# A two-layer network in fp32 on one core: Lora's products beside the convolutions, other accumulators for the outer products, and rows ordered by batch

## The chip, the cores and the metric

The kernel runs on one core of one Trainium2 chip. The metric is device time in microseconds of one execution, the median of several. Engines are named as the profile does: PE is TensorE (matmuls; PEld are its weight loads), DVE VectorE, ACT ScalarE, POOL GpSimd, SP SyncE, which here only starts DMAs.

## What is computed

x has 128 images of 64 channels with 1024 positions, in fp32. Two residual layers follow each other:

```
# layer 0: a 1x1 convolution whose weight is mixed for each image, then a low-rank product along the positions
att  = softmax(mlp(cond));  agg_w = einsum('bk,koi->boi', att, W);  agg_b = att @ bias_k
x = x + (einsum('boi,bih->boh', agg_w, x) + agg_b) @ (A @ B.T).T + bias
# layer 1: a grouped convolution (9 taps, 4 groups of 16 channels) plus a context of the image ...
y = conv1d(x, w9, groups=4, padding=4) + ctx[:, :, None] + s[None, :, None]
# ... then W_up (1024 x 1024) and the Lora product of the expert with the largest logit
base  = y @ W_up.T
delta = lora_B[e] @ (lora_A[e] @ y),   e = argmax(y @ gate_w.T + expert_bias)
x = x + base + delta
```

## The kernel before, in words

Two images (2 x 64 channels = 128 rows) are a pair `pr`, two pairs are a tile of rows `r`, and two tiles are a group `d`: 64 pairs, 32 tiles, 16 groups. All engines' orders are written out by hand (`manual_schedule`), so the order of statements is the order on each engine's queue. Within a group the loop over d (from L1005 on) weaves three things.

**W_up in seven products.** The product with W_up is done in the Strassen way: a group's y is a 2 x 2 of blocks, and seven outer products (`Outer`, i = 0 to 6), each again a Winograd scheme of seven inner products, replace eight and eight. POOL forms the sums of y: `gather` (S, L634) and `inner` (s0 to s3, L649). An inner product (`product`, L653) is two matmuls of 128 rows by 256 columns, which fp32 turns into four in the profile; in outer products 0 to 3 some are 292 wide, since 36 columns of the gate and of lora_A ride along. The accumulators are four PSUM banks: `pa` in a pool with one buffer, and `t0` to `t2`, of which an outer product takes two in turn (`product_bank`, L124). ACT copies one accumulator onto another (L686, L697, L706) and the fifth product aside (v, L694), DVE adds v and adds the accumulators to the rows of x (`evict`, L666; the helper `combine`, L211, records all these). `rest` (L689) calls the next outer product's `first` before its own last product, and `hooks` at the points a to d, where other work is put in. `spread` (L684) copies `first`'s product into `pa`, so it waits until DVE has emptied the one `pa`.

**Layer 0 and the convolution of the next group.** `in_rows` (L804: 8 accumulating products per pair, L480), `mix_rows` (L795, L490), `out_rows` (L799: two 512-wide products per pair, L511, added to x by DVE, L512). x then goes to DRAM (L513) and comes back (L520, L521) with 8 phases and 16 channels on the partitions, into one of three tiles X. `conv_rows` (L780) then fills six PSUM banks: `shared_in` twice (pm, L556: 8 matmuls of 64 by 128 each, 16 in the profile), `conv_in` four times (pc, L594, fed by POOL's `differences`, L548 and L549), with `shared_out` (m, L571 on DVE, copied to the other half by ACT, L574) between them, and at the end four `conv_out` (yt, L606 on DVE). A convolution's matmul writes 128 neighbouring columns of its bank, one group after the other, and y's rows hold the two images as neighbours, so that `conv_out` writes every eighth element.

**Gate and Lora.** After the second outer product of a pair (0 and 1, 2 and 3) `gate` (L725) picks the expert on DVE, in the free columns of one of the t banks; `turn` (L754) transposes the chosen part on PE, and `lora` (L761) makes four products of 32 rows by 512 columns (L766) into four banks, which DVE adds to x (L768). Then the rows go out (`store`, L770).

Everything else in PSUM (pxb, pz, pd, pm, pc, pzt, pl) takes the banks of the pool `ps`, of which there are four. In the loop the order on PE was: outer 0, in_rows, outer 1, out_rows, outer 2, in_rows, Lora of the first tile, outer 3, out_rows, outer 4, conv_rows of the next group's first tile, outer 5, Lora of the second tile, outer 6, conv_rows of the next group's second tile.

Of the kernel before, what the change touches and what calls it, by code (L numbers as in the profile page):

```python
# [41 lines left out]
P = 128  # L42
# [54 lines left out]
def block(ctx: ExitStack, tc: tile.TileContext, a: dict, out: bass.AP):  # L97
# [5 lines left out]
    psa = ctx.enter_context(tc.tile_pool(name="psa", bufs=1, space=PSUM))  # L103
# [17 lines left out]
    T = [pst.tile([P, N], F32, tag=f"t{i}", name=f"t{i}") for i in range(3)]  # L121
    turns = [0]

    def product_bank():  # L124
        turns[0] += 1
        return T[(turns[0] - 1) % 3]

# [171 lines left out]
    nc.gpsimd.memset(att, 0.0)  # L299
    ones = const.tile([P, 8], F32, name="ones")  # L300
    nc.gpsimd.memset(ones, 1.0)
    rank = const.tile([P, E], F32, name="rank")
    for e in range(E):
        nc.gpsimd.memset(rank[:, e : e + 1], float(E - e))

    sel = const.tile([P, FIRST, CH, 2], F32, name="sel")
    nc.vector.tensor_copy(
        sel,
        ident[:, : 2 * FIRST].rearrange("p (t b) -> p t b", b=2).unsqueeze(2).to_broadcast([P, FIRST, CH, 2]),
# [6 lines left out]
    def load_cond(g):  # L316

        if g * GP >= FIRST:
            bds[g] = BD[g % NBD]
            for b in range(2):  # L320
                nc.sync.dma_start(
                    bds[g].rearrange("(r two) t b o -> two r t b o", two=2)[b, :, :, b, :],
                    aggd.rearrange("(t two) r o -> two r t o", two=2)[b, :, g * GP : (g + 1) * GP],
                )
            load_rows(g, aggbs, aggbd, "ab")
# [21 lines left out]
    def spare(j, name):  # L347

        if j == 0:
            return psa.tile([P, N], F32, tag="pa", name=name)  # L350
        return T[j - 1]

# [48 lines left out]
    def own_att(pr):  # L401

        p = bank(f"pattx{pr}")
        nc.tensor.matmul(p[:, :8], sel[:, pr].rearrange("p o b -> p (o b)"), att[:, 0, :8], start=True, stop=True)
        attx[pr] = const.tile([P, 8], F32, name=f"attx{pr}")
        nc.vector.tensor_copy(attx[pr], p[:, :8])
# [78 lines left out]
    def layer0_mix(pr):  # L485
# [6 lines left out]
        to = z0.rearrange("k (o b) -> k b o", b=2)  # L492
        pzv = pz[:, :P].rearrange("k (b o) -> k b o", b=2)
# [7 lines left out]
    def layer0_out(pr, then=None, later=False):  # L501
        x, z0 = xs[pr], z0s.pop(pr)
        xt = X[pr % NX]
        d = x1d.tile([Q, P, P], F32, tag="x1d", name=f"x1d{pr}")
        dv = d.rearrange("q (c g) m -> (q c) g m", g=BG)
        h = P // 2
        for hf in range(2):
            cols = slice(hf * 512, (hf + 1) * 512)
            qs = slice(hf * Q // 2, (hf + 1) * Q // 2)
            pd = bank(f"pd{pr}_{hf}")  # L510
            nc.tensor.matmul(pd, z0, at[:, cols], start=True, stop=True)  # L511
            nc.vector.tensor_tensor(x[:, cols], pd, x[:, cols], ALU.add)  # L512
            nc.sync.dma_start(  # L513
                d[qs].rearrange("q r m -> r q m"), x[:, cols].rearrange("r (q m) -> r q m", m=P)
            )
        if then:
            then()

        def back():
            nc.sync.dma_start(xt[h:, :, :P], dv[:h])  # L520
            nc.sync.dma_start(xt[:h, :, 1 : P + 1], dv[h:])  # L521

        if later:
            return back
        back()

    def blocks(pr, b, g, first):

        skip = first // 2
        run = X[pr % NX][:, 2 * g + b, skip : skip + P]  # L530
        return run.rearrange("p (m two) -> p two m", two=2)[:, first - skip]

    def by_group(v):
        return v.rearrange("m (g q o) -> m g q o", g=NGC, q=Q)

    def context(pr, b, rows=slice(0, P)):
        v = ctxs[pr // GP][rows, pr % GP, b].rearrange("m (g o) -> m g o", g=NGC)
        return v.unsqueeze(2).to_broadcast([v.shape[0], NGC, Q, GC])
# [12 lines left out]
    def shared_in(pr):  # L551

        pm = bank(f"pm{pr}")
        for g in range(NGC):
            for b in range(2):
                nc.tensor.matmul(  # L556
                    pm[b * H : (b + 1) * H, g * P : (g + 1) * P],
                    blocks(pr, b, g, 1),
                    wsum[:, g],
                    start=True,  # L560
                    stop=True,
                )
        pms[pr] = pm

    def shared_out(pr):
# [3 lines left out]
        for b in range(2):  # L569
            half = slice(b * H, (b + 1) * H)  # L570
            nc.vector.tensor_tensor(by_group(m2[half, b]), by_group(pm[half]), context(pr, b, half), ALU.add)  # L571
# [5 lines left out]
    def conv_in(pr, b):  # L577

        pc = pcs[pr, b] = bank(f"pc{pr}_{b}")
        for g in range(NGC):  # L580
            cols = slice(g * P, (g + 1) * P)
            if pr < PLAIN:
                for s in range(2):
                    for o in range(2):
                        nc.tensor.matmul(
                            pc[o * H : (o + 1) * H, cols],
# [5 lines left out]
            else:  # L592
                for o in range(2):
                    nc.tensor.matmul(  # L594
                        pc[o * H : (o + 1) * H, cols],
                        diffs[pr][:, 2 * g + b, o],
# [5 lines left out]
    def conv_out(pr, b):  # L602
        if pr % 2 == 0 and b == 0:
# [3 lines left out]
            yt.rearrange("m q (o g two) -> m two g q o", two=2, g=NGC)[:, b],  # L607
            by_group(pcs.pop((pr, b))),
            context(pr, b) if pr < PLAIN else by_group(m2s[pr][:, b]),
# [8 lines left out]
    class Outer:  # L618
        def __init__(self, d, i):
            self.d, self.i, self.n = d, i, NG if i < GATES else NQ  # L620
            self.name = f"{d}_{i}"
            self.last_of_gate = i < GATES and i % 2 == (1 if d else 0)

# [31 lines left out]
        def gated(self, k, p):  # L655
            if self.i < GATES:
                r = self.i // 2
                if self.last_of_gate:
                    to = gate_part(r, 0, 3 * GL)
                else:  # L660
                    if r not in zslots[self.d]:
                        zslots[self.d][r] = sp.tile([P, 3 * GL], F32, tag="zs", name=f"zs{self.d}_{r}")
                    to = zslots[self.d][r]
# [14 lines left out]
        def first(self):  # L678
            self.t1 = product_bank()
            if self.last_of_gate:  # L680
                gate_bank[self.i // 2] = T[turns[0] % 3]
            self.product(self.t1[:, : self.n], self.unit(0, 0), held(self.i, 0), True)

        def spread(self):  # L684
            self.pa = psa.tile([P, N], F32, tag="pa", name=f"pa{self.name}")
            nc.scalar.copy(self.pa[:, :NQ], self.t1[:, :NQ])  # L686
            self.gated(2, self.t1)

        def rest(self, then, hooks):  # L689
            self.t2 = product_bank()  # L690
            wt = WT[self.i]
            self.product(self.t2[:, :NQ], self.s[0], wt[:, 1], True)
            v = tmp.tile([P, NQ], F32, tag="v", name=f"v{self.name}")
            nc.scalar.copy(v, self.t2[:, :NQ])  # L694
            hooks("a")
            self.product(self.pa[:, :NQ], self.s[1], wt[:, 2])
            nc.scalar.copy(self.t2[:, :NQ], self.pa[:, :NQ])  # L697
            hooks("b")
            self.product(self.t1[:, : self.n], self.unit(0, 1), held(self.i, 1))
            self.gated(0, self.t1)  # L700
            self.evict(self.t1[:, :NQ], 1)
# [3 lines left out]
            self.product(self.t2[:, : self.n], self.s[2], held(self.i, 2))  # L705
            nc.scalar.copy(self.pa[:, NQ:], self.t2[:, :NQ])  # L706
            both = self.pa.rearrange("p (k n) -> p k n", k=2)
            combine(nc.vector, both, both, "+", v.unsqueeze(1).to_broadcast([P, 2, NQ]))
# [3 lines left out]
            self.product(self.t2[:, : self.n], self.unit(1, 1), held(self.i, 3))  # L712
            if then:
                then.spread()
            self.gated(1, self.t2)
            self.evict(self.t2[:, :NQ], 2)

    zslots = {}
    gate_bank = {}

    def gate_part(r, first, n):

        return gate_bank[r][:, NG + first : NG + first + n]

    def gate(d, r):  # L725

        zs = zslots[d].pop(r)
        z = gate_part(r, 0, 3 * GL)
        z2 = sp.tile([P, GL], F32, tag="z2", name=f"z2{d}_{r}")
        nc.vector.tensor_tensor(z2, z[:, 2 * GL :], zs[:, 2 * GL :], ALU.add)  # L730
        nc.vector.tensor_tensor(z[:, : 2 * GL], z[:, : 2 * GL], zs[:, : 2 * GL], ALU.add)
        nc.vector.tensor_tensor(z[:, GL : 2 * GL], z[:, GL : 2 * GL], z2, ALU.add)  # L732
        pv = z[:, : 2 * GL].rearrange("p (t n) -> p t n", t=2)
        lg, sc = (gate_part(r, 3 * GL + 2 * E * k, 2 * E).rearrange("p (t e) -> p t e", t=2) for k in range(2))
# [45 lines left out]
    def conv_rows(r):  # L780

        a, b = pairs(r)
        shared_in(a)
# [115 lines left out]
    zslots[0] = {}  # L899
# [6 lines left out]
    o[0, 1].spread()  # L906
    o[0, 1].rest(o[0, 0], steps(wb[0], {"a": 1, "b": 2, "c": 2, "d": 1}))
# [8 lines left out]
    conv_rows(1)  # L916
# [11 lines left out]
    o[0, 3].spread()  # L928
    wb[2] = w_block(2, (0, 1, 3))
# [65 lines left out]
    zslots[1] = {}  # L995
# [9 lines left out]
    for d in range(1, ND):  # L1005
        more = d + 1 < ND
        r0, r1 = 2 * d + 2, 2 * d + 3
        if more:
            for i in range(7):
                o[d + 1, i] = Outer(d + 1, i)  # L1010
            zslots[d + 1] = {}
# [22 lines left out]
        else:  # L1034
            conv_rows(2 * d + 1)
# [9 lines left out]
        zms[0] = gate(d, 0)  # L1045
        if more:
            out_rows(r0)

# [11 lines left out]
        q[2].rest(q[3], hook({"c": [turn0]} if more else {}))  # L1060
        if more:
            in_rows(r1)
            lora(d, 0, zts[0])
# [8 lines left out]
        zms[1] = gate(d, 1)  # L1072
        if not more:
            lora(d, 0, zts[0])
        if more:
            back = out_rows(r1, True)

# [10 lines left out]
        q[4].rest(q[5], hook({"c": [turn1]} if more else {}))  # L1088
        if more:
            conv_rows(r0)  # L1090
            back()

# [19 lines left out]
        q[5].rest(q[6], nothing)  # L1112
        if d + 2 < ND:
            lora(d, 1, zts[1])
# [8 lines left out]
        q[6].rest(o[d + 1, 0], nothing)  # L1123
        if d + 2 < ND:
            store(d, 1)
            conv_rows(r1)
        else:
            lora(d, 1, zts[1])
            store(d, 1)


def _by_rows(v):

    v = v.reshape(2, NGC, GC, *v.shape[2:])
    return np.moveaxis(v, (2, 1, 0), (0, 1, 2)).reshape(P, *v.shape[3:])
# [93 lines left out]
```

## Time and profile before

| what | value |
|---|---|
| median of 3 runs (lowest to highest) | 1224.99 us (1223.98 to 1226.67) |
| the profiled execution's own time | 1229.31 us |
| span in its profile | 1227.3 us |
| PE, DVE, POOL, ACT busy | 98%, 68%, 64%, 26% of the span |
| granted TensorE clock | 0.997 of full |
| DMA | 277.58 MB, mean 226 GB/s |

The profile comes from one execution, which took 1229.31 us; the span lies within it. A line of the time line gives start and duration in us, engine, line of the kernel, operation, written and read tiles, partitions x elements of the operands, and how many instructions are merged into it; in square brackets stands how long the engine was idle before it and what ended that. Ends of matmuls are modelled, so start to start tells more of PE than durations do.

### The profile page before, as it was taken

The page shows a single profiled execution, that of the slowest core. Times are in us where ns is not written, and L with a number is a line of the kernel's source. Part 1 is how long each engine was busy: PE and PEld are TensorE (multiplying, and loading weights), DVE is VectorE, ACT ScalarE, POOL GpSimd, SP SyncE. Part 2 cuts the span into 40 slices and gives each one's busy share as a digit, 9 for nine tenths or more (in the row PEclk, how much of TensorE's full clock was granted, in tenths as well). Part 3 has the DMA queues.
Part 4 walks back from the last instruction along what each step waited for, and adds up shares of the span by engine and source line. Part 5 has one row for each costly group of instructions (what it writes and reads, how often), then busy time and mean ns, then how long its engine had stood idle before and what let it go on. Part 6 is the DMA issues. An engine that isn't in the chain of part 4 may idle for free.

```text
span 1227.3 us, 22059 instructions
## 1 busy us (share of the span) xinstructions
PE 1204.6 (98%) x8007; PEld 967.5 (79%) x8007; DVE 833.4 (68%) x1699; ACT 314.7 (26%) x927; POOL 786.8 (64%) x749
## 2 busy tenths in 40 slices
PE   8889999999999999999999999999999999999998
PEld 6756878888787888878888787788878878788876
DVE  6768757676675767667676675767667576675765
ACT  3324322222132222213222232222213222132221
POOL 2478568756667676567756657766567756657753
PEclk9989999999999999999999999999999999999999
DMA  8976877677786677777677686767777676686633
GB/s 297 290 281 167 277 236 225 224 221 247 217 247 204 186 278 210 232 240 228 224 218 252 208 258 206 209 249 205 232 243 224 230 216 253 206 245 219 178 134 132
DMA packets 200939, 277.58 MB, mean 226 GB/s; under 512 B 18304, under 2 KB 159232, under 8 KB 200832
## 3 DMA queue, kind: packets, MB, share of 16 engines
q1 hardware_dynamic: 168304, 127.12, 36.9%
q10 hardware_dynamic: 32528, 149.06, 35.3%
q8 instruction: 64, 1.05, 0.4%
q14 instruction: 43, 0.35, 0.1%
HBM read 201.36 MB, written 74.78 MB: 225 GB/s over the span
## 4 chain that ended last, share of the span: by engine, by line
PE 90%; DMA 4%; issue 2%; DVE 2%; POOL 1%; ACT 1%; SPq 0%; ACTq 0%; DVEq 0%; POOLq 0%
PE t L653 40%; PE pa L653 15%; PE pxb L480 9%; PE pd L511 9%; PE pc L594 8%; PE pm L556 4%; PE pl L766 3%; DMA X<-x1d 1%; PE pz L490 1%; DMA wp<-in_wq 1%; POOL s L211 1%; DMA x1d<-xr 1%; DMA ctxd<-ctx 1%; POOL S L211 1%; DVE xr L211 0%
## 5 line engine op out<-in xcount | busy, mean ns | idle before, releaser
L211 DVE TENSOR_TENSOR xr<-xr,t 128x256 f32<-128x256 f32 x384 | 146.9, 417 | 148.3 <-ACT t L664 103.5
L653 PE MATMUL pa<-wt,s 128*128 128x256 f32 x896 | 230.4, 380 | 1.6 <-POOL S L211 1.3
L775 POOL TENSOR_TENSOR xr<-xr,ffn_bias 128x1024 f32<-128x1024 f32 x61 | 142.7, 2362 | 137.9 <-DVE xr L211 66.9
L211 POOL TENSOR_TENSOR S<-yt,yt 128x1024 f32<-128x1024 f32 x48 | 113.6, 2366 | 153.9 <-PE t L653 153.9
L653 PEld LDWEIGHTS pa<-wt,s 128*128 128x128 f32 x896 | 165.2, 190 | 32.3 <-issue 2.4
L211 DVE TENSOR_TENSOR pa<-pa,v 128x512 f32<-128x512 f32 x112 | 78.3, 699 | 139.6 <-ACT pa L706 139.6
L653 PE MATMUL t<-wp,S 128*128 128x256 f32 x576 | 142.7, 379 | 0.4 <-ACT pa L706 0.4
L480 PEld LDWEIGHTS pxb<-B,xt 128*128 128x128 f32 x1024 | 122.9, 196 | 12.4 <-DVE t L732 5.3
L480 PE MATMUL pxb<-B,xt 128*128 128x128 f32 x1024 | 124.0, 280 | 6.5 <-DVE t L732 4.9
L211 DVE TENSOR_TENSOR xr<-xr,pa 128x512 f32<-128x512 f32 x192 | 124.8, 684 | 3.9
L653 PEld LDWEIGHTS t<-wp,S 128*128 128x128 f32 x576 | 109.5, 190 | 17.4 <-ACT pa L706 0.8
L653 PE MATMUL t<-wt,s 128*128 128x256 f32 x448 | 121.8, 394 | 1.3 <-POOL s L211 1.2
L606 DVE TENSOR_TENSOR yt<-pc,m 128x512 f32<-128x512 f32 x124 | 121.3, 1100 | 1.0
L211 POOL TENSOR_TENSOR s<-S 128x256 f32<-128x256 f32 x160 | 116.6, 729 | 5.2
L653 PEld LDWEIGHTS t<-wt,s 128*128 128x128 f32 x448 | 78.8, 190 | 51.4 <-issue 38.6
L511 PE MATMUL pd<-AT,z 128*128 128x512 f32 x256 | 116.8, 596 | 1.5 <-ACT z L496 0.8
L548 POOL TENSOR_TENSOR df<-X 128x512 f32<-128x512 f32 x62 | 64.6, 1043 | 81.7 <-DMA X<-x1d 48.3
L594 PE MATMUL pc<-ws,df 128*64 128x128 f32 x1984 | 114.3, 273 | 1.5 <-DVE wg L211 1.1
L653 PE MATMUL t<-wg,S 128*128 128x292 f32 x384 | 111.2, 413 | 0.5 <-POOL S L211 0.5
L768 DVE TENSOR_TENSOR xr<-pl,xr 128x512 f32<-128x512 f32 x128 | 79.5, 683 | 46.8 <-PE pl L766 46.8
L594 PEld LDWEIGHTS pc<-ws,df 128*64 128x64 f32 x1984 | 109.4, 137 | 2.3 <-POOL df L549 1.3
L653 PE MATMUL t<-wg,yt 128*128 128x292 f32 x384 | 110.2, 410 | 0.5 <-ACT pa L706 0.5
(147 smaller groups left out, 1670.7 us busy)
## 6 DMA issues: line engine op xcount, KB each, us to landing
wt<-wd ACTq DMA_DIRECT2D x105, 768.0 KB, 4.7
x1d<-xr SPq DMA_DIRECT2D x128, 256.0 KB, 3.5
X<-x1d SPq DMA_DIRECT2D x128, 256.0 KB, 4.3
out<-xr SPq DMA_DIRECT2D x31, 1024.0 KB, 6.9
xr<-in_x ACTq DMA_DIRECT2D x28, 1024.0 KB, 7.8
xt<-in_xt ACTq DMA_DIRECT2D x55, 512.0 KB, 8.6
wd<-wt ACTq DMA_DIRECT2D x7, 768.0 KB, 4.7
xt<-in_xt SPq DMA_DIRECT2D x9, 512.0 KB, 7.0
```

Source lines behind the costliest of these rows:

```text
L211: eng.tensor_tensor(to, x, y, ALU.add if op == "+" else ALU.subtract)
L480: nc.tensor.matmul(pxb[:, :P], xt[:, c, :], bt[:, c, :], start=(c == 0), stop=(c == NC - 1))
L490: nc.tensor.matmul(pz[:, :P], xbs.pop(pr), bd.rearrange("p b o -> p (b o)"), start=True, stop=not first)
L511: nc.tensor.matmul(pd, z0, at[:, cols], start=True, stop=True)
L548: nc.gpsimd.tensor_tensor(diffs[pr][:, :, 0], at_even, at_odd, ALU.subtract)
L556: nc.tensor.matmul(pm[b * H : (b + 1) * H, g * P : (g + 1) * P], blocks(pr, b, g, 1), wsum[:, g], start=True, stop=True,)
L594: nc.tensor.matmul(pc[o * H : (o + 1) * H, cols], diffs[pr][:, 2 * g + b, o], ws[:, g, o], start=True, stop=True,)
L606: nc.vector.tensor_tensor(yt.rearrange("m q (o g two) -> m two g q o", two=2, g=NGC)[:, b], by_group(pcs.pop((pr, b))), context(pr, b) if ...
L653: nc.tensor.matmul(p, lhs[:, c], w[:, c], start=fresh and c == 0, stop=c == 1, skip_group_check=True)
L766: nc.tensor.matmul(p, zt[rows, :], lb[rows, :], start=True, stop=True)
L768: nc.vector.tensor_tensor(x, p, x, ALU.add)
L775: eng.tensor_tensor(xs[pr], xs[pr], fbias, ALU.add)
```

## The change

- **Accumulators.** `psa` is gone. The fourth bank is U, which all outer products share; an outer product's `t` turns through the three T, and its `pa` is the T that the one before used as `t`. The product that uses `pa` comes first in `rest`, the product for v (`fifth`) goes to a bank of `ps` and moves behind the second use of `t`. The gate's parts accumulate in U over two products (ACT zeroes them first in outer products of an even or odd number, by group), and the gate works in a bank of `ps`, with one DVE operation less and some small ACT copies more.
- **Order.** In the loop, conv_rows of the next group's first tile moves behind outer product 5, and both Loras move directly ahead of a conv_rows (their first `pm` then goes to U). Outer product 5 follows 4 directly. `gate` moves behind `out_rows`, its transpose from hook c to hook d. In the last group there is no such convolution, and Lora stays between outer products. The first group's order stays, but for the place of `fifth`.
- **Rows.** x's, y's and the context's rows are ordered image, channel in group, group. A convolution's matmul now writes every fourth column of its bank, the groups interleaved; `conv_out` writes runs of 64 elements. x goes to DRAM by image (two DMAs per pair, as before, but after both halves have been added), and comes back in four DMAs per pair in place of two.

The diff, cut to its core:

```diff
-    psa = ctx.enter_context(tc.tile_pool(name="psa", bufs=1, space=PSUM))
     T = [pst.tile([P, N], F32, tag=f"t{i}", name=f"t{i}") for i in range(3)]
+    U = pst.tile([P, N], F32, tag="u", name="u")
...
-            nc.sync.dma_start(
-                d[qs].rearrange("q r m -> r q m"), x[:, cols].rearrange("r (q m) -> r q m", m=P)
-            )
+        for b in range(2):
+            nc.sync.dma_start(
+                d[b].rearrange("q c g m -> (c g) q m"),
+                x[b * CH : (b + 1) * CH].rearrange("r (q m) -> r q m", m=P),
+            )
...
         def back():
-            nc.sync.dma_start(xt[h:, :, :P], dv[:h])
-            nc.sync.dma_start(xt[:h, :, 1 : P + 1], dv[h:])
+            for b in range(2):
+                dv = d[b].rearrange("q c g m -> (q c) g m")
+                own_ = slice(b * NGC, (b + 1) * NGC)
+                nc.sync.dma_start(xt[h:, own_, :P], dv[:h])
+                nc.sync.dma_start(xt[:h, own_, 1 : P + 1], dv[h:])
...
+    def by_phase(v):
+        return v.rearrange("m (q n) -> m q n", q=Q)
+
+    def of_group(v, g):
+        return v.rearrange("m (n g) -> m g n", g=NGC)[:, g]
...
-                    pm[b * H : (b + 1) * H, g * P : (g + 1) * P],
+                    of_group(pm[b * H : (b + 1) * H], g),
                     blocks(pr, b, g, 1),
                     wsum[:, g],
-                    start=True,
+                    start=g == 0,
...
-                        pc[o * H : (o + 1) * H, cols],
-                        diffs[pr][:, 2 * g + b, o],
+                        of_group(pc[o * H : (o + 1) * H], g),
+                        diffs[pr][:, NGC * b + g, o],
...
         nc.vector.tensor_tensor(
-            yt.rearrange("m q (o g two) -> m two g q o", two=2, g=NGC)[:, b],
-            by_group(pcs.pop((pr, b))),
-            context(pr, b) if pr < PLAIN else by_group(m2s[pr][:, b]),
+            yt[:, :, b * CH : (b + 1) * CH],
+            by_phase(pcs.pop((pr, b))),
+            context(pr, b) if pr < PLAIN else by_phase(m2s[pr][:, b]),
...
         def first(self):
-            self.t1 = product_bank()
+            k = turns[0]
+            turns[0] += 1
+            self.t, self.pa = T[k % 3], T[(k - 1) % 3]
...
+        def fifth(self):
+            m5 = bank(f"m5{self.name}")
+            self.product(m5[:, :NQ], self.s[0], WT[self.i][:, 1], True)
+            self.v = tmp.tile([P, NQ], F32, tag="v", name=f"v{self.name}")
+            nc.scalar.copy(self.v, m5[:, :NQ])
...
         def rest(self, then, hooks):
-            self.product(self.t2[:, :NQ], self.s[0], wt[:, 1], True)
-            nc.scalar.copy(v, self.t2[:, :NQ])
-            hooks("a")
             self.product(self.pa[:, :NQ], self.s[1], wt[:, 2])
-            nc.scalar.copy(self.t2[:, :NQ], self.pa[:, :NQ])
+            nc.scalar.copy(U[:, :NQ], self.pa[:, :NQ])
+            if self.first_of_gate:
+                nc.scalar.copy(U[:, NQ:NG], none)
+            hooks("a")
+            self.product(self.t[:, : self.n], self.unit(0, 1), held(self.i, 1))
+            self.gated(0, self.t)
+            self.evict(self.t[:, :NQ], 1)
             hooks("b")
-            self.product(self.t1[:, : self.n], self.unit(0, 1), held(self.i, 1))
-            self.gated(0, self.t1)
-            self.evict(self.t1[:, :NQ], 1)
+            if not self.v:
+                self.fifth()
             hooks("c")
...
-    def conv_rows(r):
+    def conv_rows(r, first=U):
         a, b = pairs(r)
-        shared_in(a)
+        shared_in(a, first)
...
-        zms[0] = gate(d, 0)
         if more:
             out_rows(r0)
+        zms[0] = gate(d, 0)
...
-        q[2].rest(q[3], hook({"c": [turn0]} if more else {}))
+        q[2].rest(q[3], hook({"d": [turn0]} if more else {}))
         if more:
             in_rows(r1)
-            lora(d, 0, zts[0])
...
-        q[4].rest(q[5], hook({"c": [turn1]} if more else {}))
-        if more:
-            conv_rows(r0)
-            back()
-
+        q[4].rest(q[5], hook({"d": [turn1]} if more else {}))
...
         q[5].rest(q[6], nothing)
+        lora(d, 0, zts[0])
+        conv_rows(r0)
+        back()
         if d + 2 < ND:
-            lora(d, 1, zts[1])
             load_cond(r0 + 2)
...
         q[6].rest(o[d + 1, 0], nothing)
+        lora(d, 1, zts[1])
+        store(d, 1)
         if d + 2 < ND:
-            store(d, 1)
             conv_rows(r1)
```

## Prediction, made before the changed kernel was run

> **What bounds the kernel now.** I read the page first (busy shares, slices, chain), then the busy time of each engine in three stretches, then TensorE's waits in the middle stretch, then the time line around the places that the change moves.
>
> ```profile
> PE 1204.6 (98%) x8007; PEld 967.5 (79%) x8007; DVE 833.4 (68%) x1699; ACT 314.7 (26%) x927; POOL 786.8 (64%) x749
> ...
> PE 90%; DMA 4%; issue 2%; DVE 2%; POOL 1%; ACT 1%; SPq 0%; ACTq 0%; DVEq 0%; POOLq 0%
> ```
>
> The first line is the engines' busy time, the second the chain of work that ended last, by engine. The next is the stretch from 174 to 1129 us: its length, then busy time (and instructions) of PE, PEld, DVE, ACT and POOL, granted clock, DMA share, GB/s.
>
> ```profile
> 174.00:1129.00 955.00, 955.00 (x6422) 773.29 (x6421) 644.88 (x1313) 235.20 (x702) 632.13 (x585) 1.00 0.74 228
> ```
>
> PE is busy for all of its 955 us, DVE for 645, POOL for 632; asked for PE's waits in that stretch, the trace lists none. So thirteen periods (one per group d; the same rows come back every 73.5 us) hold no gap on PE. Nothing is won there by making another engine faster; a change gains only if PE's own stream gets shorter, and any wait that it adds is paid in full. Since matmul ends are modelled, I go by starts.
>
> **What Lora costs today.** The rows: start, duration, engine, line.
>
> ```profile
> 642.85 1.89 PE L653 MATMUL t<-wp,S 128*128 128x256 f32 x8
> ...
> 644.67 1.14 PE L766 MATMUL pl<-lb,zt 32*128 32x512 f32 x8
> ...
> 645.74 1.13 PE L653 MATMUL t<-wt,s 128*128 128x256 f32 x4
> 645.83 2.49 DVE L768 TENSOR_TENSOR xr<-pl,xr 128x512 f32<-128x512 f32 x4 [0.63 <-PE pl L766]
> ...
> 646.71 1.03 PE L653 MATMUL pa<-wt,s 128*128 128x256 f32 x4
> ```
>
> An undisturbed product of four 256-column matmuls takes 0.86 to 0.87 us from start to start (617.37 to 618.23 in the next rows). Lora's matmuls use 32 of the 128 rows of the array, four at once. Entering costs 644.67-642.85-2x0.865 = 0.09 us, the products 1.07 (645.74-644.67), and the first full product after them takes 0.97, so leaving costs 0.11. That is 1.27 us for the second Lora of a group. The first one stands behind layer0_in and needs banks that ACT still empties; its rows are these:
>
> ```profile
> 614.93 1.55 PE L766 MATMUL pl<-lb,zt 32*128 32x512 f32 x8
> 616.40 1.13 PE L653 MATMUL t<-wt,s 128*128 128x256 f32 x4
> 617.37 1.03 PE L653 MATMUL pa<-wt,s 128*128 128x256 f32 x4
> 618.23 1.15 PE L653 MATMUL t<-wg,S 128*128 128x292 f32 x4
> ```
>
> It takes 1.47 plus 0.09 and 0.11, that is 1.67. In both, DVE starts adding the four results 1.16 us after the first matmul (645.83-644.67) and is at it for 2.49 us.
>
> **What a convolution costs today.**
>
> ```profile
> 633.04 1.97 PE L556 MATMUL pm<-wsum,X 128*64 128x128 f32 x32
> ...
> 633.74 0.74 DVE L211 TENSOR_TENSOR xr<-xr,t 128x256 f32<-128x256 f32 x2
> ...
> 634.41 2.84 DVE L571 TENSOR_TENSOR m<-pm,cx 64x512 f32<-64x512 f32 x4
> ...
> 634.84 3.66 PE L594 MATMUL pc<-ws,df 128*64 128x128 f32 x64
> ...
> 637.27 3.92 DVE L606 TENSOR_TENSOR yt<-pc,m 128x512 f32<-128x512 f32 x4
> ...
> 638.43 1.13 PE L653 MATMUL t<-wt,s 128*128 128x256 f32 x4
> ```
>
> Six banks are filled, 0.90 us each: two pm, then four pc. The sixth takes the bank of the second pm, so it waits until DVE's fourth m is done. It starts at 633.04+5x0.90 = 637.54, m ends at 634.41+2.84 = 637.25: hidden, with 0.29 us to spare. What happens without that cover is in the last group, where DVE began later:
>
> ```profile
> 1175.02 2.81 PE L594 MATMUL pc<-ws,df 128*64 128x128 f32 x48
> 1175.19 2.84 DVE L571 TENSOR_TENSOR m<-pm,cx 64x512 f32<-64x512 f32 x4
> ...
> 1178.18 1.10 PE L594 MATMUL pc<-ws,df 128*64 128x128 f32 x16 [0.34 <-DVE m L571]
> ```
>
> m ends at 1178.03, PE goes on at 1178.18: 0.15 us from DVE's end to PE. PE was due at 1175.02+3x0.90 = 1177.72, so it lost 0.46.
>
> **Part 1, Lora directly ahead of conv_rows** (14 first Loras, d = 1 to 14; 13 second ones, d = 1 to 13). One change of array shape goes away on each side, and the first Lora no longer waits for ACT: without a new wait the pair would take 1.07 + s + 5.40 us, s being the direct change from row tiles to column tiles, in place of 1.67 or 1.27 plus 5.40. The trace has no such change; the nearest rows give 0.09 to 0.11, nothing is the other end. But DVE's four additions now stand in its queue ahead of the four m. With Lora's first matmul at 0: additions 1.16 to 3.65; m from 3.57 (DVE overlaps such operations by 0.07, as 633.74+0.74 against 634.41) to 6.41; the sixth bank from 6.56. In the changed program the sixth bank is still that of the second pm; the first pm goes to U, which DVE has emptied by then (the like operation before a convolution ends at 634.48 above, and with one destination in place of two still 0.3 earlier, against 1.07 us of Lora on PE). PE alone would be there at 1.07+s+4.50 = 5.57+s, so s is hidden up to 0.99, and PE waits. From Lora's start to the sixth bank: 6.56, against 4.50 plus the old Lora: 6.56-4.50-1.67 = +0.39, and 6.56-4.50-1.27 = +0.79. Sum: 14x0.39 + 13x0.79 = **+15.7 us**. The other banks come free in time (the last addition ends at 3.65, the fifth bank is due at 4.67).
>
> **Part 2, the accumulators.** Matmul counts stay. Outer products 4 and 5 now follow each other directly, so the cover of a convolution is gone there. By the rows: pa's copy (ACT, 0.36) starts 0.25 after its product, ends at 0.61 and reaches PE 0.15 later, inside the 0.86 of the product between. DVE's chain for one outer product (v added 0.70, two 512-wide and two 256-wide additions) ends 3.3 us after the product that starts it; the copy into U waits for it and is done at 3.9, and the first product that needs it is due at 4.3. So no new stall: 0, but at slacks of 0.1 to 0.4. In the last group, which has no filler, the old rotation stalls:
>
> ```profile
> 1187.14 1.10 PE L653 MATMUL pa<-wt,s 128*128 128x256 f32 x4 [0.28 <-ACT zs L664]
> ...
> 1194.23 1.10 PE L653 MATMUL t<-wt,s 128*128 128x256 f32 x4 [1.19 <-POOL s L211]
> ...
> 1210.81 1.10 PE L653 MATMUL pa<-wt,s 128*128 128x256 f32 x4 [1.34 <-POOL S L211]
> ```
>
> By starts these are 0.45, 1.36 and 1.50 us late. The first and third wait for the copy into pa behind DVE's additions, and go; of the second about 0.9 goes, since it hangs on POOL, whose input the shorter conv_out gives 1.4 us earlier. **-2.9 us.** The gate loses one DVE operation (0.19) and moves behind layer0_out: DVE ends it at about 6.4 us after pd's first matmul, its transpose is due at 6.9, hidden. ACT gains small copies; it is at 26%.
>
> **Part 3, batch outermost.** conv_out writes runs of 64 in place of every eighth element: four take 3.92 us now, four contiguous ones of that size 2.49 (the additions above). That spares DVE 1.4 us per convolution, 45 in all, after the wait of part 1, so it is worth 0. POOL's differences keep their size. The way back from DRAM takes 4 DMAs per pair of images in place of 2: 128 more issues on SP at 0.52 us each, which delay store and load_cond behind them by 1 us; the store is still issued over 10 us before the load into its rows. X of the fourth pair lands some 5 us after the first pm, 8 us before its use. 0; in the first 100 us, where DMA is 88% busy, up to 1 us either way.
>
> The price that no row shows is pm and pc written to PSUM at every fourth element. Lower end: no change, 0.90 us a bank (below nothing is excluded: as many columns pass). Upper end: as DVE fares in SBUF, 3.92/2.49 = 1.57 times, 1.41 us a bank. Lora's start to the sixth bank is then 1.07+5x1.41 = 8.12, and that bank 0.51 longer: +2.46 and +2.86 a pair, 14 and 13 times, and 6x0.51 for each of the 4 convolutions without Lora, +84 in all. I take the lower end: the nearest row is that of the same matmuls into the same memory, DVE's has another engine and another memory, and up to 1.2 times is hidden behind the DVE wait anyway (5x1.08+1.07 = 6.5).
>
> Against it stands a rule of the Trainium skill, "PSUM — Partial Sum Buffer", Specifications: PSUM's lines are 8 bytes, and any non-contiguous pattern slows matmuls significantly. No run here shows it; if it doubles a bank's time (an estimate from two fp32 values to a line), the sum is +156 in place of +13.
>
> **Sum.** The profiled execution took 1229.31 us (span 1227.3), 4.3 above the median of the three runs, 1224.99. +15.7-2.9 = +12.8: 1242.1 for such an execution, **1238** for the median.
>
> **Rivals.**
> *No wait at the sixth bank* (DVE gets through m sooner than I reckon, or PE doesn't need that bank): PE's stream shortens by 14x(0.60-s) + 13x(0.20-s), 11 us at s = 0, 8 at 0.11; with the tail 14 and 11: **1211 to 1214**, faster. For it: m may run like other additions, since its context operand becomes one run. Against: m's four rows take 2.84 in every convolution, and the 0.34 us wait stands in the trace.
> *Half of it:* m shrinks to 2.49 us. Then 6.2 in place of 6.56, 27x0.35 = 9.5 less: **1228**.
> *Strided PSUM writes cost:* at the upper end 1225+84-2.9 = **1306**, slower for another reason. It decides from 1.2 times the present 0.90 us on; at 1.25 it would be about 1253.
>
> **How the numbers follow.** Forecast 0.60 (own range 1230 to 1244); no wait 0.12; half of it 0.09; strided writes 0.19, a few hundredths of it below 1250 and some of it above 1306. A measurement here tells 0.2% (2.4 us) from no change. Faster 0.13, same 0.07 (part of the half case, 1228 being 0.25% up), slower 0.80. The range takes the first three and the mild end of the last: 1210 to 1250.
>
> **What would show it.** Right: in each period PE waits about 0.9 us ahead of the second pc of the second pair, released by DVE's m; from Lora's first matmul to that bank 6.5 us; pm and pc still at 0.90 us a bank; yt at about 0.62 us each; no waits of pa. Wrong: PE's list of waits stays empty between 174 and 1129 (first rival), or banks of 1.4 us and more (strided writes), or waits of pa or u between outer products 4 and 5, which part 2 excludes.

## The result and the profile after

The changed kernel takes **1245.08 us** (median of 4 runs, 1243.96 to 1246.70); the kernel before took 1225.79 in the same session (4 runs). The ratio is 1.016, 95% interval 1.0141 to 1.0179: slower by 1.6%. The profiled execution took 1246.70 us, its span is 1244.9, its granted clock 0.995. The forecast was 1238, with a range of 1210 to 1250; 1245 lies inside it and 1 us above the narrower 1230 to 1244 that the prediction gave its main case.

First the page of the changed kernel: the engines' busy time and the chain by engine.

```profile
PE 1199.9 (96%) x8007; PEld 967.8 (78%) x8007; DVE 780.6 (63%) x1667; ACT 328.6 (26%) x959; POOL 787.6 (63%) x750
...
PE 85%; DVE 7%; DMA 4%; issue 2%; POOL 1%; ACT 0%; SPq 0%; ACTq 0%; DVEq 0%; POOLq 0%
```

DVE has 53 us less to do than before and yet its share of the chain has gone from 2 to 7%: less busy, more often the one waited for. PE is busy for less of a longer span. The next view is the middle stretch, with its length and then the busy time of PE, PEld, DVE, ACT and POOL, granted clock, DMA share and GB/s:

```profile
174.00:1140.00 966.00, 943.85 (x6388) 765.96 (x6387) 596.27 (x1271) 244.38 (x720) 626.63 (x583) 1.00 0.70 223
```

PE, which had no gap here before, now lacks 22 us. Asked for PE's waits in that stretch, the trace of before listed none; the changed one lists a single row (line, releaser, us in total, times, longest):

```profile
PE pc L595 <- DVE m L573: 22.2, 26, 0.9
```

That is twice per group for 13 groups. The time line around one of them, columns as in the prediction:

```profile
437.90 1.14 PE L770 MATMUL pl<-lb,zt 32*128 32x512 f32 x8
438.01 0.42 DVE L207 TENSOR_TENSOR xr<-xr,u 128x256 f32<-128x256 f32 x1
438.98 1.10 PE L557 MATMUL u<-wsum,X 128*64 128x128 f32 x16
439.06 2.48 DVE L772 TENSOR_TENSOR xr<-pl,xr 128x512 f32<-128x512 f32 x4 [0.63 <-PE pl L770]
439.90 1.07 PE L557 MATMUL pm<-wsum,X 128*64 128x128 f32 x16
440.78 2.82 PE L595 MATMUL pc<-ws,df 128*64 128x128 f32 x48
441.47 1.40 DVE L573 TENSOR_TENSOR m<-u,cx 64x512 f32<-64x512 f32 x2
442.89 1.41 DVE L573 TENSOR_TENSOR m<-pm,cx 64x512 f32<-64x512 f32 x2
444.33 2.48 DVE L607 TENSOR_TENSOR yt<-pc,m 128x512 f32<-128x512 f32 x4
444.45 1.09 PE L595 MATMUL pc<-ws,df 128*64 128x128 f32 x16 [0.85 <-DVE m L573]
445.47 1.13 PE L656 MATMUL t<-wt,s 128*128 128x256 f32 x4
```

Read it down the DVE rows: Lora's four additions (439.06 to 441.54), then the four m, and the last m ends at 444.30. On PE u is followed by pm after 0.92 us and pm by the first pc after 0.88; by the starts of their single matmuls the three pc take 0.873 us each. So PE is due at 440.78+3x0.873 = 443.40, and it starts the sixth bank at 444.45, 1.05 us late. (The list gives 0.85, since it counts from the modelled end of the last matmul.)

To see where the 17.7 us of span come from I added up, for every matmul, the time from its start to the next matmul's start. Per period (13 of them, from the first layer0_out of group 1 to that of group 14), in us:

| time ahead of the next matmul, after a matmul of | before | after | difference |
|---|---|---|---|
| pc | 7.19 | 9.39 | +2.20 |
| pl (Lora) | 2.55 | 2.14 | -0.41 |
| outer products | 44.94 | 44.66 | -0.28 |
| pxb | 7.24 | 7.14 | -0.09 |
| pm (and its U), pd, pz, pzt | 11.57 | 11.57 | 0 |
| sum | 73.49 | 74.91 | +1.42 |

The convolutions' pc lose 2.20 a period and everything else gains 0.78. Over the 13 periods the net loss is 18.4 us. The first 163 us add 2.8, the stretch from there (first layer0_out of group 14) to the last matmul loses 4.0, and what follows the last matmul's start adds 0.45.

### The profile page after: what moved, and what is told of

Read it like the earlier page. It is cut to its first block, busy times and chain, and to the rows that moved or that the text cites. A ratio compares the mean times of both kernels' runs of the same rounds, so it can differ in the third digit from the quotient of the medians.

```text
span 1244.9 us, 22049 instructions
## 1 busy us (share of the span) xinstructions
PE 1199.9 (96%) x8007; PEld 967.8 (78%) x8007; DVE 780.6 (63%) x1667; ACT 328.6 (26%) x959; POOL 787.6 (63%) x750
## 3 DMA queue, kind: packets, MB, share of 16 engines
q8 instruction: 64, 1.05, 0.4%
## 4 chain that ended last, share of the span: by engine, by line
PE 85%; DVE 7%; DMA 4%; issue 2%; POOL 1%; ACT 0%; SPq 0%; ACTq 0%; DVEq 0%; POOLq 0%
PE t L656 32%; PE u L656 16%; PE pxb L476 8%; PE pd L504 8%; PE m L656 8%; PE pc L595 6%; DVE m L573 4%; PE pl L770 3%; DVE xr L772 2%; PE pm L557 1%; DMA X<-x1d 1%; PE pz L486 1%; PE u L557 1%; DMA xt<-in_xt 1%; DMA ctxd<-ctx 1%
## 5 line engine op out<-in xcount | busy, mean ns | idle before, releaser
L207 DVE TENSOR_TENSOR xr<-xr,t 128x512 f32<-128x512 f32 (+1 forms) x384 | 197.9, 550 | 176.5 <-ACT zs L663 153.0
L656 PE MATMUL t<-wt,s 128*128 128x256 f32 x896 | 233.8, 383 | 0.0
L207 DVE TENSOR_TENSOR t<-t,v 128x512 f32<-128x512 f32 x112 | 78.3, 699 | 195.4 <-ACT t L710 195.4
L656 PEld LDWEIGHTS t<-wt,s 128*128 128x128 f32 x896 | 164.9, 190 | 41.3 <-issue 20.3
L656 PE MATMUL m<-wt,s 128*128 128x256 f32 x448 | 115.1, 379 | 0.1
L576 ACT COPY m<-m 64x512 f32<-64x512 f32 x124 | 76.5, 617 | 145.2 <-DVE m L573 138.3
L656 PEld LDWEIGHTS m<-wt,s 128*128 128x128 f32 x448 | 85.0, 190 | 16.1 <-POOL s L207 0.5
L505 DVE TENSOR_TENSOR xr<-pd,xr 128x512 f32<-128x512 f32 x128 | 85.8, 687 | 11.8 <-PE pd L504 8.5
L504 PEld LDWEIGHTS pd<-AT,z 128*128 128x128 f32 x256 | 48.0, 190 | 50.8 <-issue 36.6
L207 POOL TENSOR_TENSOR S<-yt 128x1024 f32<-128x1024 f32 x32 | 75.5, 2358 | 16.1 <-PE pz L490 16.1
```

The source lines that it names most:

```text
L207: eng.tensor_tensor(to, x, y, ALU.add if op == "+" else ALU.subtract)
L576: nc.scalar.copy(m2[other, b], m2[half, b])
L656: nc.tensor.matmul(p, lhs[:, c], w[:, c], start=fresh and c == 0, stop=c == 1, skip_group_check=True)
```

## Experiments

The theory: all of the loss is one wait, and it is an order on DVE. The sixth bank is that of the second pm, and DVE releases it with the last of four m, which now stand behind Lora's four additions. The rivals are the strided PSUM writes, DVE's changed amount of work, and the new rotation. The runs came in two sessions; the kernel before took 1224.83 in the first (7 runs) and 1226.18 in the second (17 runs).

### The other pair's m first

```diff
         conv_in(a, 0)
-        shared_out(a)
+        shared_out(b if first else a)
         conv_in(a, 1)
-        shared_out(b)
+        shared_out(a if first else b)
```

> The changed kernel, with DVE's two m of the second pair put ahead of the two of the first pair wherever the first pm lies in U. The sixth bank is that of the second pm, so it comes free after two m in place of four. Theory (the four additions of Lora ahead of the four m in DVE's queue hold the sixth bank): from Lora's first matmul the bank is free at 3.57 + 1.41 + 0.15 = 5.13 us, PE is due there at 5.57, so the wait of 0.9 us is gone from PE's list: 6.55 - 5.57, and 0.12 for starting again, times 27 pairs, 30 us less, about 1215, below the kernel before by some 10. Rival (the rotation of the accumulators or the rows cost the time, and the wait only shows it): another wait takes its place, and the time stays above 1235.

Measured: 1217.83 us (1217.48 to 1217.94), ratio 0.9943 (0.9929 to 0.9958). Nothing is taken away from DVE; only which pm it empties first is changed, and U, which no matmul of the convolution needs again, comes last. Its time line:

```profile
429.12 1.14 PE L770 MATMUL pl<-lb,zt 32*128 32x512 f32 x8
...
431.99 3.69 PE L595 MATMUL pc<-ws,df 128*64 128x128 f32 x64
432.68 1.40 DVE L573 TENSOR_TENSOR m<-pm,cx 64x512 f32<-64x512 f32 x2
...
434.10 1.41 DVE L573 TENSOR_TENSOR m<-u,cx 64x512 f32<-64x512 f32 x2
...
435.61 1.13 PE L656 MATMUL t<-wt,s 128*128 128x256 f32 x4
```

From Lora's start to the next product it is now 6.49 us (435.61-429.12), 7.57 in the changed kernel. The four pc banks are one row of 64 matmuls without a gap. pm is free at 434.08; PE needs it at 431.99+3x0.873 = 434.61. Seven of the 13 periods take 72.73 or 72.74 us (the mean of all 13 is 72.88), against 73.48 in nearly all of before and 74.88 in most of the changed kernel: 0.74 shorter than the one, 2.14 shorter than the other. The wait was the whole loss per period, and the rest of the change is a small gain.

### One more operation ahead of the m

```diff
+    more_work = const.tile([P, N], F32, name="more_work")
...
         conv_in(a, 0)
+        if first:
+            nc.vector.tensor_tensor(more_work, at[:, :N], at[:, N:], ALU.add)
         shared_out(a)
```

> The changed kernel, with one more DVE operation (128 x 512, both operands in SBUF, its result unused) in front of the four m of every convolution that has its first pm in U. Theory: whatever stands there on DVE reaches PE in full, 27 times. By the 128 x 1024 addition of the bias (1.90 us) it takes some 0.9 us, so 24 us more, about 1269, and the wait at the sixth bank grows from 0.9 to about 1.8. Rival (the change from Lora's tiles to the convolution's, or PE itself, holds that bank): no change, 1245.

Measured: 1268.47 us (1265.61 to 1268.87), ratio 1.0352 (spans 1266.5 against 1244.9). PE's loss follows the dose. The first view is PE's waits in the middle stretch, the second the time line with the added operation.

```profile
PE pc L596 <- DVE m L574: 41.9, 26, 1.8
```

```profile
442.16 0.99 DVE L792 TENSOR_TENSOR more_work<-AT 128x512 f32<-128x512 f32 x1
443.08 1.40 DVE L574 TENSOR_TENSOR m<-u,cx 64x512 f32<-64x512 f32 x2
...
446.07 1.09 PE L596 MATMUL pc<-ws,df 128*64 128x128 f32 x16 [1.77 <-DVE m L574]
```

Here the m start 0.92 us later (0.61 in the group's other convolution, where the added operation takes 0.68 us), the wait grows from 0.85 to 1.77, and ten of the 13 periods take 76.40 to 76.46 us: +1.52 on 74.88, which is 0.92+0.61 within a hundredth. What stands on DVE ahead of the m is paid in full. Three periods are 1.7 to 1.9 us longer still, and that is another matter. Two neighbouring periods in the stretch view (columns as above):

```profile
464.30:540.70 76.40, 73.19 (x495) 59.30 (x494) 47.62 (x102) 18.94 (x56) 49.15 (x46) 1.00 0.69 220
540.70:618.80 78.10, 74.88 (x495) 60.54 (x494) 48.00 (x102) 18.94 (x56) 50.08 (x48) 0.98 0.67 213
```

DVE and ACT do nearly the same, but the granted clock is 0.98. The time line of PE finds the place, directly behind one of the waits:

```profile
598.93 1.09 PE L596 MATMUL pc<-ws,df 128*64 128x128 f32 x16 [1.76 <-DVE m L574]
599.96 1.94 PE L657 MATMUL t<-wt,s 128*128 128x256 f32 x4
601.69 2.07 PE L657 MATMUL t<-wg,yt 128*128 128x292 f32 x4
```

The outer products step at 0.43 us a matmul in place of 0.21, for some 3.4 us. The three such periods make up 5.3 of the 21.6 us of added span. So it was luck that the time met the expectation: 0.9 had been expected of the added operation in every convolution, it costs 0.61 in half of them, and the slow stretches made up for that.

### Neighbouring columns in PSUM

```diff
     def of_group(v, g):
-        return v.rearrange("m (n g) -> m g n", g=NGC)[:, g]
+        return v[:, g * P : (g + 1) * P]
```

> The changed kernel, but the convolutions' matmuls write 128 neighbouring columns of a bank again, while DVE reads as if they were interleaved; so the order of y's channels does not fit and the output is not the reference's. Everything else costs the same. Theory (writes at every fourth column cost PE nothing here): a bank stays at 0.9 us, the time at 1245 within 2.5. Rival (they cost something that the trace hides in the wait): the fifth bank ends earlier, and the four convolutions without Lora get shorter; at 1.2 times it would be 4 us less.

Measured: 1245.86 us (1242.98 to 1247.3), ratio 1.0177 to before. The period is 74.908, the changed kernel's to the third digit, and the wait is the same, as its time line shows:

```profile
437.07 2.82 PE L595 MATMUL pc<-ws,df 128*64 128x128 f32 x48
...
440.75 1.09 PE L595 MATMUL pc<-ws,df 128*64 128x128 f32 x16 [0.85 <-DVE m L573]
```

The wait on DVE could hide a small slowdown of these banks, so the table above is the sharper witness: the time after pm's matmuls, ahead of which nothing waits, is 3.602 us per period in the kernel before (neighbouring columns) and in the changed one (every fourth). This rival is out.

### conv_out with its old pattern

Shown for the pairs from PLAIN on; the first pairs keep the new pattern:

```diff
         nc.vector.tensor_tensor(
-            yt[:, :, b * CH : (b + 1) * CH],
-            by_phase(pcs.pop((pr, b))),
-            context(pr, b) if pr < PLAIN else by_phase(m2s[pr][:, b]),
+            yt.rearrange("m q (o g two) -> m two g q o", two=2, g=NGC)[:, b],
+            by_group(pcs.pop((pr, b))),
+            by_group(m2s[pr][:, b]),
             ALU.add,
```

> The changed kernel, but conv_out of the pairs from PLAIN on writes every eighth element as in the kernel before (the order of channels in the output is then not the reference's): four conv_out take about 3.9 us again in place of 2.48. Theory (conv_out stands behind the m that PE waits for, and nothing waits for yt soon): the same time as the changed kernel, 1243 to 1248. Rival (DVE's 1.4 us per convolution matter): 26x1.4 = 36 us more at the most, 1255 to 1281.

Measured: 1243.75 us (1243.26 to 1244.84), ratio 1.0153 (1.0136 to 1.0171). Its period is 74.907. Its conv_out take the old time again:

```profile
442.51 3.90 DVE L611 TENSOR_TENSOR yt<-pc,m 128x512 f32<-128x512 f32 x4
442.62 1.09 PE L595 MATMUL pc<-ws,df 128*64 128x128 f32 x16 [0.85 <-DVE m L573]
```

So the 1.4 us that the new row order takes off each convolution on DVE are worth nothing: they lie behind the m, and nobody waits for them.

### Lora away from the convolutions again

The first Lora goes back to its old place; the second goes between outer products 4 and 5 (it was between 5 and 6), since a convolution now stands behind 5.

```diff
             in_rows(r1)
+            lora(d, 0, zts[0])
...
+        if more:
+            lora(d, 1, zts[1])
         w_fetch(6)
...
         q[5].rest(q[6], nothing)
-        lora(d, 0, zts[0])
         conv_rows(r0)
...
         q[6].rest(o[d + 1, 0], nothing)
-        lora(d, 1, zts[1])
```

> The changed kernel, with both Loras taken away from the convolutions: the first behind the second in_rows, as in the kernel before, the second between outer products 4 and 5. Rotation, rows and the place of the convolutions stay as changed. Theory: no wait at the sixth bank, the period goes from 74.9 us back to 73.5, 14 times 1.4 less, about 1225, so equal to the kernel before within 3 us (what the first 150 us lose and the last group gains stays). Rival (rotation or rows cost it): 1240 or more, the period stays near 74.9.

Measured: 1245.23 us (1242.24 to 1246.39), ratio 1.0164 (1.0149 to 1.0179). The expectation failed by 20 us. The sixth bank indeed no longer waits, but the list of waits has two new rows:

```profile
PE u L557 <- DVE xr L207: 10.8, 21, 0.5
PE u L557 <- DMA out<-xr: 2.6, 5, 0.5
```

and the time line shows one:

```profile
437.06 1.03 PE L656 MATMUL u<-wp,S 128*128 128x256 f32 x4
...
438.12 0.42 DVE L207 TENSOR_TENSOR xr<-xr,u 128x256 f32<-128x256 f32 x1
...
438.59 1.17 PE L557 MATMUL u<-wsum,X 128*64 128x128 f32 x16 [0.51 <-DVE xr L207]
439.52 1.11 PE L557 MATMUL pm<-wsum,X 128*64 128x128 f32 x16
439.80 1.41 DVE L573 TENSOR_TENSOR m<-u,cx 64x512 f32<-64x512 f32 x2 [1.26 <-PE u L557]
...
440.39 3.73 PE L595 MATMUL pc<-ws,df 128*64 128x128 f32 x64
```

The first pm goes to U, and the outer product has just used U: DVE empties it until 438.54. In the changed kernel Lora's 1.07 us on PE cover exactly this. Taking Lora away uncovers another wait, 26 times: 0.51 us in the list, 0.58 by starts, and the convolution's last bank takes 0.07 longer besides. (The profile puts five of them down to a DMA; in all 26 PE starts 0.05 to 0.06 us after that addition of DVE ends.) The reading is tested next.

### The same, and the first pm in a pool bank

```diff
-        conv_rows(r0)
+        conv_rows(r0, None)
...
-            conv_rows(r1)
+            conv_rows(r1, None)
```

> lora_back, and conv_rows takes a pool bank for the first pm in place of U in both calls of the loop. lora_back lost 26 times 0.51 us at the first matmul into U, plus a restart. Theory (U still held by DVE's last addition of the outer product, which Lora's 1.07 us covered): these waits go, no other takes their place (the sixth bank had none in lora_back), 1245.2 - 26x(0.51 to 0.65): 1228 to 1232, that is 0.3 to 0.6% above the kernel before. Rival (the order of the outer products itself delays DVE): a wait of 0.3 us and more turns up at the sixth bank, 1236 to 1245.

Measured: 1226.27 us (1225.43 to 1228.31, 10 runs), ratio 1.0009 (0.9998 to 1.0021), 2 us below what was expected: the waits and what comes with them were worth 1.30 us a period (74.80-73.50), 17 in all, as expected at the upper end. Of the rest 1.5 lies in the first 160 us and 0.9 behind the periods. PE's list of waits in the middle stretch is empty, and the period is 73.496, that of the kernel before (73.489). The pc are one row again:

```profile
433.08 2.85 DVE L573 TENSOR_TENSOR m<-pm,cx 64x512 f32<-64x512 f32 x4 [0.64 <-PE pm L557]
433.60 3.53 PEld L595 LDWEIGHTS pc<-ws,df 128*64 128x64 f32 x64
433.71 3.66 PE L595 MATMUL pc<-ws,df 128*64 128x128 f32 x64
```

So the new rotation and the new rows, with Lora away from the convolutions and the first pm in the pool as before, are worth nothing per period.

### Lora's place alone, in the kernel before

```diff
             in_rows(r1)
-            lora(d, 0, zts[0])
...
         if more:
+            lora(d, 0, zts[0])
             conv_rows(r0)
...
-            lora(d, 1, zts[1])
             load_cond(r0 + 2)
...
+        lora(d, 1, zts[1])
+        store(d, 1)
         if d + 2 < ND:
-            store(d, 1)
             conv_rows(r1)
...
```

> The kernel before with nothing changed but the place of Lora (both calls directly ahead of the convolution in the groups 1 to 13); accumulators and rows stay as they were. Theory (the wait of the sixth bank behind DVE comes from Lora's place alone): the PE stream gets 1.3 to 1.42 us longer in each of the 13 periods, so 1224.8 + 13x1.3 to 13x1.42, with half a microsecond from group 14: 1242 to 1244; PE waits some 26 times about 0.9 us ahead of pc for DVE's m. Rival (the wait comes from the new rotation or from the rows): 1224.8 - 13x0.4 to 0.6, 1216 to 1220, and no such wait.

Measured: 1250.37 us (1249.2 to 1250.5), ratio 1.0207 (1.0192 to 1.0222). Right in kind, 6 us outside in size, and not by the wait that was expected:

```profile
PE pm L556 <- DVE xr L768: 22.5, 26, 1.0
```

```profile
434.11 1.14 PE L766 MATMUL pl<-lb,zt 32*128 32x512 f32 x8
...
435.27 2.48 DVE L768 TENSOR_TENSOR xr<-pl,xr 128x512 f32<-128x512 f32 x4 [0.63 <-PE pl L766]
436.02 1.97 PE L556 MATMUL pm<-wsum,X 128*64 128x128 f32 x32 [0.77 <-DVE xr L768]
...
437.82 3.94 PE L594 MATMUL pc<-ws,df 128*64 128x128 f32 x64
...
441.69 1.13 PE L653 MATMUL t<-wt,s 128*128 128x256 f32 x4
```

Lora fills all four banks of the pool, so without U the first pm has to wait until DVE has done Lora's first addition; the pc after it, 3.87 us to the next product in place of 3.59, hold a little of the old wait besides. Lora ahead of a convolution costs 1.77 us a period with the old accumulators and rows (75.26 against 73.49), and 1.42 in the changed kernel, where the first pm goes to U. U spares the wait for Lora's first bank, and the order of the m is what makes the new place pay.

### The better version, with the start mended

This is m_b_first with two edits: x goes to DRAM after each half again (of all pairs, not of the first alone, and in four DMAs a pair in place of two), and the two convolutions without a Lora ahead take a pool bank:

```diff
             nc.vector.tensor_tensor(x[:, cols], pd, x[:, cols], ALU.add)
+            qs = slice(hf * Q // 2, (hf + 1) * Q // 2)
+            for b in range(2):
+                nc.sync.dma_start(
+                    d[b, qs].rearrange("q c g m -> (c g) q m"),
+                    x[b * CH : (b + 1) * CH, cols].rearrange("r (q m) -> r q m", m=P),
+                )
... (the two DMAs behind both halves go)
-    conv_rows(2)
+    conv_rows(2, None)
...
-    conv_rows(3)
+    conv_rows(3, None)
```

> m_b_first with two edits in the first 160 us: x goes to DRAM after each half as in the kernel before, and the two convolutions without a Lora ahead of them (groups of r = 2 and 3) take a bank for the first pm in place of U. Theory: the two waits for U there (0.67 and 0.51 us) go and X lands a little sooner: 1215 to 1217, against 1217.83 for m_b_first. Rival (the first 160 us are set by DMA and scatter by more than that): 1217 to 1219.

Measured: 1214.76 us (1212.67 to 1215.69, 6 runs), ratio 0.9916 (0.9903 to 0.9929): the fastest of all, 30 us below the changed kernel, and just under the 1215 to 1217 that were expected. The two waits for U in the start (0.67 and 0.51 us) are gone. Of the rest I claim no cause: the waits of pm for X there were 2.2 us in m_b_first and 2.4 here, and the time of the first layer0_out of group 1 varies between 158.7 and 163.1 us among the seven other profiles whose first 160 us are ordered as in the changed kernel (160.0 here). That earlier stores help is not shown.

## Why the prediction was right, and where its sizes were off

**The bound and "any wait is paid in full": right.** PE's waits (22 us in the list) cost 2.20 us a period at pc, and what the change saves elsewhere, 0.78, is all that stands against it; dve_more and yt_every_eighth are the two sides of it, one operation ahead of the m costing its whole time, 1.4 us behind them costing none.

**Part 1, the mechanism: right to a hundredth.** From Lora's start to the sixth bank: 444.45-437.90 = 6.55, predicted 6.56. Lora itself is 1.07 in both places, the direct change to column tiles costs nothing that the rows show (the last pl to u takes 0.52 us, as the last pl to t does), and the saving outside pc is 0.78 per period; the prediction's saving without a wait comes to 0.60+0.20 = 0.80 at s = 0, and m_b_first, which has no wait at the sixth bank, shows 0.74.

**Part 1, the size: a term was too small.** The prediction took 0.90 us for every bank. That is the mean of the six. By the starts of single matmuls, in the undisturbed convolutions of before, the first bank takes 0.93, the next four 0.87 each and the last, up to the next product, 0.97. Five banks are therefore 4.42 us and not 4.50, and PE is due at the sixth earlier than the prediction had it: it is late by 1.05 where 0.99 was reckoned. The sixth bank itself then takes 1.02 (444.45 to 445.47), 0.05 more than undisturbed. That is 0.11 per convolution, 2.9 us for the 26 of them, nearly all of the 3.1 us by which the 13 periods exceed the forecast. The 1.02 stood in the trace of before: the last group's bank in the second fence on what a convolution costs began at 1178.18 behind a wait, and the next product starts at 1179.20. A typical period is 74.88 against 73.48, +1.40 (mean +1.42), in place of +1.18.

**Part 2, no new stalls: right, for a reason that the order gave.** No pa or u waits between outer products 4 and 5. That U is free for the first pm "against 1.07 us of Lora on PE" was the cover named, and lora_back shows it being needed: 0.5 us late without it. In the two convolutions of the first group, which have no Lora ahead, the wait does show (0.67 and 0.51 us), and the prediction had not looked there.

**Part 2, the tail: under-sized.** The outer products of the last group lose 4.05 us in place of 2.9: the stall behind POOL's s goes as a whole (1.36, of which 0.9 had been counted), and one of 0.23 that was not on the list goes too. Another 0.28 is what these products also save in every period. Against it pc rises by 0.51: the new wait comes once more (14 first Loras, 13 periods), and the old one of the last group goes.

**Part 3: right.** conv_out 2.48 and worth 0; strided PSUM writes at 0.90 a bank. The Trainium skill, "PSUM — Partial Sum Buffer", Specifications, says that a non-contiguous pattern slows matmuls significantly. For fp32 with every fourth column no run here shows it (3.602 us per period for the pm in both kernels; 1245.86 against 1245.08), and the measurement decides. (What the prediction would have added for a doubled bank, +156, leaves out the -2.9 of part 2: with it some +153.)

**The start: 0, up to 1 either way, was forecast; +2.8 in this profile.** The two waits for U explain 1.3 of it, and the first Lora gives 0.5 back. pm's waits for X grow from 0.9 to 1.9 us. Whether the change does that is open: the seven profiles that start in this order, the changed kernel's 163.1 the latest of them, come to this point between 158.7 and 163.1 us, and before at 160.3.

**The sum.** Predicted +12.8 on the profiled execution, measured +17.7 on the span: +3.1 in the periods, +2.8 in the start, -1.5 in the tail, +0.45 after the last matmul's start. For the median, taking off the 4.3 us by which the profiled execution of before exceeded its median took off too much; the changed kernel's profiled execution is 1.6 above its median.

**The rivals.** The time of "no wait at the sixth bank" (1211 to 1214) is nearly reached, but only by reversing the m (1217.83). "Half of it" needed m at 2.49 us; they take 2.83.

## What to carry to other kernels

When work moves next to other work on a full engine, list what comes with it on the other engines' queues, and ask which of those operations frees the next buffer: here the same eight DVE operations in another order are worth 27 us out of 1245. A buffer that nobody needs soon should be emptied last. And when something is taken out of a full stream, ask what it covered: Lora hid the emptying of U, and taking it back only traded one wait for another.

## What the runs showed of the hardware

- In dve_more, the kernel with the longest waits, PE ran at half its pace for some 3.4 us in three of the 13 periods, with 1.7 to 1.9 us lost each time (granted clock 0.98 over the period). All three places follow one of its 13 waits of 1.75 to 1.77 us; the ten others, and the waits of 1.46, were followed by nothing of the kind. In the changed kernel, whose waits are 0.85, no period is over 0.2 us longer than the others. The Trainium skill, "TensorE: Matmul & The Clock Gate", Part 1, has a gate that watches activity in free-running windows of about 3.4 us and halves the clock after an idle one; the length agrees with these rows, while here the halving followed waits of half a window, and not always. What decides is not shown.
- A wait costs PE more than the idle time listed for it. Behind a listed 0.85 us the bank starts 1.05 us late by starts: a matmul of these banks is listed as 0.27 us long, while two start every 0.109. The bank behind the wait takes 1.02 us against 0.97 in before; but that last bank takes 1.00 in m_b_first and 1.04 in lora_back with no wait ahead of it, so this 0.05 is not shown to come from the wait.
- Matmuls that write every fourth fp32 column of a PSUM bank run as fast as those that write neighbours (3.602 us for four banks in both).
- DVE writing 512 fp32 per partition in runs of 64 takes 2.48 us for four, and at every eighth element 3.90; the same sums, so the pattern alone costs 0.36 us each.
- The m, each on 64 partitions and on the other half of them than the one before, follow each other on DVE without overlap (two in 1.40 us, 0.70 each), while Lora's additions on all 128 partitions and as many columns overlap (four in 2.48 us, with 0.60 from start to start). Whether the number of partitions or the change of half does it is not shown.
